# Attention times value in four 32-column tiles, two attention visits per group, and the projections reordered around them

## The chip, the cores and the metric

The kernel runs on one core of a Trainium2 chip, in true float32. The metric is the device time of one execution, in microseconds (us). TensorE is the matrix engine; VectorE (DVE), ScalarE (ACT) and GpSimd (POOL) work beside it.

## The reference, cut to what matters

Two layers on 64 graphs of 256 nodes and 512 features, each layer with a norm, a ReLU and a residual. The first mixes nodes with the adjacency matrix, the second is masked attention with 8 heads of 64.

```python
# layer 0
h = jnp.maximum(_layernorm(x), 0.0)
y = jnp.einsum('nm,bmd->bnd', adj, h)
x = x + jnp.einsum('bnd,do->bno', y, weight) + bias
# layer 1
h = jnp.maximum(_layernorm(x), 0.0)
q, k, v = ...                                   # h @ Wq + bq etc., 8 heads of 64
scores = jnp.einsum('bqhd,bkhd->bhqk', q, k) / sqrt(64)
scores = scores + (1.0 - adj) * -1e9
attn = jax.nn.softmax(scores)
out = jnp.einsum('bhqk,bkhd->bqhd', attn, v)
x = x + out @ Wo + bo
```

## The kernel before

It takes two graphs at a time: 32 groups, one after the other, software-pipelined by hand. The names in the profile are `py` (adjacency times h), `w` (layer 0's projection), `ph` (transposes of h), `q`, `k`, `v`, `sc` (scores), `pav` (attention times value), `pden` (the softmax denominators, a matmul with ones) and `o` (the output projection, called post). Group numbers stand in the names: `o_9a` is bank a of group 9's post.

A projection is done by a seven-product scheme on halves: five projections, seven products each, eight passes of TensorE for each product. It steps through its products, and other work is put between the steps. The order of `read` and `finish` in it, which are adds on VectorE for `w` and `o`, decides when an accumulation bank comes free:

```python
def project(s, halves, by_token, name, read, finish):
    pa = new("a")
    product(pa, s, "a11", halves, "b11", by_token, stop=False)   # first product
    u1 = read(pa, 1)                                             # w, o: residual add
    yield
    ...                                                          # second product, bank b
    product(pa, s, "s2", halves, "t2", by_token, start=False, stop=False)  # third, into pa again
    u2 = read(pa, 2)
    yield
    pc = new("c")
    product(pc, s, "s1", halves, "t1", by_token, stop=False)
    yield
    product(pa, s, "s3", halves, "t3", by_token, start=False)
    u3 = read(pa, 3)              # w, o: two residual adds
    give(pa)
    finish(pc, u3, 1, 1)
    yield
    ...                           # sixth product, bank d
    product(pc, s, "s4", halves, "b22", by_token, start=False)   # last: waits for finish(pc)
```

Attention goes by pairs of heads, so four times per group. `attend` uses two 64-column tiles of TensorE for a pair; behind it stand the scores of the next pair, and that whole stretch (`pav`, `pden`, `sc`) I call a visit.

```python
def attend(g, hp):
    po = bank([P, GN], f"pav_{g}_{hp}")
    pd = bank([P, GN], f"pden_{g}_{hp}")
    for b in range(GB):
        for k in range(NT):
            for j in range(2):
                h = 2 * hp + j
                nc.tensor.matmul(po[j * HD:(j + 1) * HD, b * N:(b + 1) * N], V..., a[:, j * NT + k, :], ...)
    for b in range(GB):
        for j in range(2):
            nc.tensor.matmul(pd[j * HD:(j + 1) * HD, b * N:(b + 1) * N], ones, s[:, j, :], ...)
    ...
    nc.scalar.activation(den, pd, AF.Identity, accum_out=stats[:, 0, i:i + 1])   # frees pd
    def invert(c):                                                               # four times
        nc.vector.reciprocal(rden[:, c * P:(c + 1) * P], den[:, c * P:(c + 1) * P])
    def divide():
        nc.vector.tensor_tensor(o, po, rden, op=ALU.mult)
    for c in range(4):
        after(1 + c, invert, c)       # so many steps later, among other work
    after(5, divide)

SHARE = (11, 3, 12, 7)                # steps of the next group's layers behind each visit
for g in range(NG):
    for hp in range(4):
        attend(g, hp)
        score(g, hp + 1)              # or score(g + 1, 0)
        ...                           # behind visit 1: post(g - 1)
        for _ in range(steps):
            run(layers)
```

## Time and profile before

| what | before |
|---|---|
| median time | 2965.51 us (2964.91 to 2967.16) |
| TensorE busy | 98% |
| period of a group, from `py` to the next `py` | 90.3 us |
| one visit: `pav` + `pden` + `sc` | 1.78 + 0.96 + 1.93 us |
| start: until `py` of group 2 begins | 189.8 us |
| end: from `py` of group 31 | 156.0 us |

An engine's row in the profile gives its busy time, its share of the span and its number of instructions. In the timeline each row is a block of equal instructions: start, duration, engine, source line, operation and tiles, shapes, count, and in brackets how long the engine stood idle before the block and whose instruction ended that. Ends of matmuls are modelled, so the cost of a block is the distance from its start to the next start. The chain is the work that ended last, followed back step by step to what released it. A weight load is exposed when no running matmul covers it, as at 1020.29 us in this profile: the load for `w_11c` begins 0.25 us after the last matmul ended, and the second pass starts 0.32 us after the first, where those behind it stand 0.216 apart. The prediction below shows the rows.

### The profile page before, as it was taken

The page shows a single profiled execution, that of the slowest core. Times are in us where ns is not written, and L with a number is a line of the kernel's source. Part 1 is how long each engine was busy: PE and PEld are TensorE (multiplying, and loading weights), DVE is VectorE, ACT ScalarE, POOL GpSimd, SP SyncE. Part 2 cuts the span into 40 slices and gives each one's busy share as a digit, 9 for nine tenths or more (in the row PEclk, how much of TensorE's full clock was granted, in tenths as well). Part 3 has the DMA queues.
Part 4 walks back from the last instruction along what each step waited for, and adds up shares of the span by engine and source line. Part 5 has one row for each costly group of instructions (what it writes and reads, how often), then busy time and mean ns, then how long its engine had stood idle before and what let it go on. Part 6 is the DMA issues. An engine that isn't in the chain of part 4 may idle for free.

```text
span 2964.6 us, 39918 instructions
## 1 busy us (share of the span) xinstructions
PE 2896.8 (98%) x15632; PEld 2341.8 (79%) x15632; DVE 1698.0 (57%) x2959; ACT 942.4 (32%) x1697; POOL 1886.4 (64%) x1754
## 2 busy tenths in 40 slices
PE   7899999999999999999999999999999999999997
PEld 6688788878887887888888888888878878888885
DVE  3465556555555655555555556555556555665554
ACT  2233333333323333333333233333333333333331
POOL 6566656666666666566666666665666665666653
PEclk9899999999999999999999999999999999999998
DMA  3000000000000000000000000000000000000000
GB/s 125 1 1 29 29 29 29 15 15 29 29 29 29 1 29 29 29 29 24 6 29 29 29 29 5 25 29 30 29 29 1 29 29 29 29 14 16 29 15 30
DMA packets 39279, 75.74 MB, mean 26 GB/s; under 512 B 3248, under 2 KB 3504, under 8 KB 39088
## 3 DMA queue, kind: packets, MB, share of 16 engines
q1 hardware_dynamic: 39088, 73.15, 6.9%
q8 instruction: 125, 2.05, 0.3%
q14 instruction: 66, 0.54, 0.1%
HBM read 39.59 MB, written 33.55 MB: 25 GB/s over the span
## 4 chain that ended last, share of the span: by engine, by line
PE 93%; DVE 5%; POOL 1%; issue 0%; ACT 0%; DMA 0%; SPq 0%; ACTq 0%; POOLq 0%; DVEq 0%
PE sc L587 8%; PE pav L618 8%; PE py L469 8%; DVE x L424 4%; PE pden L624 4%; PE ph L511 2%; PE q_1a L383 0%; POOL a L595 0%; DVE rden L637 0%; DMA adj_sb<-in_adj_dram 0%; PE q_31a L383 0%; PE q_30a L383 0%; PE q_23a L383 0%; PE q_20a L383 0%; PE q_19a L383 0%
## 5 line engine op out<-in xcount | busy, mean ns | idle before, releaser
L595 POOL TENSOR_TENSOR a<-a,top 128x1024 f32<-128x1024 f32 x256 | 598.5, 2359 | 342.9 <-DVE a L592 342.9
L592 DVE SCALAR_TENSOR_TENSOR a<-sc,maskT 128x512 f32<-128x512 f32 x512 | 318.1, 684 | 370.1 <-PE sc L587 370.1
L637 DVE RECIPROCAL rden<-den 128x128 f32<-128x128 f32 x512 | 453.1, 922 | 5.2 <-ACT den L633 5.2
L607 POOL TENSOR_TENSOR as<-a 128x512 f32<-128x512 f32 x256 | 322.9, 1273 | 33.0 <-ACT a L604 33.0
L53 POOL TENSOR_TENSOR rs<-rs,mhalf 128x2 f32<-128x2 f32 (+1 forms) x96 | 77.6, 808 | 416.4 <-DVE nb L52 416.4
L604 ACT ACTIVATE a<-a 128x1024 f32<-128x1024 f32 x256 | 266.4, 1053 | 122.5 <-POOL a L595 122.5
L618 PE MATMUL pav<-a,v 128*64 128x256 f32 x2048 | 256.8, 392 | 15.1 <-ACT a L604 15.1
L587 PE MATMUL sc<-q,k 64*128 64x256 f32 x2048 | 257.9, 392 | 0.0
L587 PEld LDWEIGHTS sc<-q,k 64*128 64x128 f32 x2048 | 188.9, 188 | 67.6 <-PE pden L624 36.9
L376 POOL TENSOR_TENSOR t_h<-h1T 128x256 f32<-128x256 f32 x128 | 92.9, 726 | 230.4 <-DVE h1T L513 230.1
L469 PE MATMUL py<-adjT,h 128*128 128x256 f32 x1024 | 231.4, 384 | 6.7 <-ACT h L441 6.7
L633 ACT ACTIVATE den<-pden 128x512 f32<-128x512 f32 x128 | 75.8, 592 | 489.5 <-PE pden L624 489.5
L618 PEld LDWEIGHTS pav<-a,v 128*64 128x64 f32 x2048 | 136.8, 138 | 118.5 <-issue 52.6
L469 PEld LDWEIGHTS py<-adjT,h 128*128 128x128 f32 x1024 | 192.9, 191 | 42.6 <-issue 10.3
L501 ACT ACTIVATE h<-x,nb,rs 128x512 f32<-128x512 f32 x128 | 97.2, 807 | 366.5 <-POOL nb L54 366.5
L443 POOL TENSOR_TENSOR x<-x,b_r 128x512 f32<-128x512 f32 x128 | 161.5, 1273 | 0.3 <-ACT h L441 0.3
L524 POOL TENSOR_TENSOR x<-x,bo_r 128x512 f32<-128x512 f32 x128 | 159.8, 1269 | 0.0
L471 ACT COPY yT<-py 128x512 f32<-128x512 f32 x128 | 75.1, 586 | 209.9 <-PE py L469 209.9
L624 PE MATMUL pden<-as,ones 128*64 128x256 f32 x1024 | 135.7, 384 | 3.5 <-POOL as L607 3.5
L624 PEld LDWEIGHTS pden<-as,ones 128*64 128x64 f32 x1024 | 78.1, 139 | 38.4 <-POOL as L607 4.4
L441 ACT ACTIVATE h<-x,nb,rs 128x512 f32<-128x512 f32 x128 | 102.8, 806 | 6.4 <-POOL nb L54 6.4
L376 POOL TENSOR_TENSOR t_y<-yT,t_y 128x256 f32<-128x256 f32 x128 | 93.3, 729 | 15.4 <-ACT yT L471 12.8
(2950 smaller groups left out, 5766.4 us busy)
## 6 DMA issues: line engine op xcount, KB each, us to landing
x<-in_x_dram SPq DMA_DIRECT2D x32, 1024.0 KB, 5.3
out_dram<-x SPq DMA_DIRECT2D x64, 512.0 KB, 2.8
w_sb<-in_L_gnn_weight_dram SPq DMA_DIRECT2D x1, 1024.0 KB, 8.0
wq_sb<-in_L_gnn_Wq_dram SPq DMA_DIRECT2D x1, 1024.0 KB, 11.4
wk_sb<-in_L_gnn_Wk_dram SPq DMA_DIRECT2D x1, 1024.0 KB, 13.3
wv_sb<-in_L_gnn_Wv_dram SPq DMA_DIRECT2D x1, 1024.0 KB, 10.9
wo_sb<-in_L_gnn_Wo_dram SPq DMA_DIRECT2D x1, 1024.0 KB, 8.9
adj_sb<-in_adj_dram SPq DMA_DIRECT2D x1, 256.0 KB, 5.9
```

The lines of the kernel that those rows point to most:

```text
L376: eng.tensor_tensor(self.t[n][:, c, :], self.operand(p, c), self.operand(q, c), op=ALU.subtract)
L443: nc.gpsimd.tensor_tensor(xt[:, t, :], xt[:, t, :], b0_r, op=ALU.add)
L469: nc.tensor.matmul(ps[:, b * N:(b + 1) * N], h[:, b * NT + k, d * P:(d + 1) * P], adjT[:, k, :], start=(k == 0), stop=(k == NT - 1))
L524: nc.gpsimd.tensor_tensor(xt[:, t, :], xt[:, t, :], bo_r, op=ALU.add)
L587: nc.tensor.matmul(ps[j][:, kt * N:(kt + 1) * N], k[j * HD:(j + 1) * HD, c, kt * P:(kt + 1) * P], q[j * HD:(j + 1) * HD, c, :], start=True ...
L592: nc.vector.scalar_tensor_tensor(a[:, j * NT:(j + 1) * NT, :].rearrange("p k n -> p (k n)"), ps[j], SCALE, maskT_f, op0=ALU.mult, op1=ALU.add)
L595: nc.gpsimd.tensor_tensor(a, a, top_b, op=ALU.subtract)
L604: nc.scalar.activation(a, a, AF.Exp)
L607: nc.gpsimd.tensor_tensor(s, a4[:, :, 0, :], a4[:, :, 1, :], op=ALU.add)
L618: nc.tensor.matmul(po[j * HD:(j + 1) * HD, b * N:(b + 1) * N], V[g][h // 4, b][:, k, (h % 4) * HD:(h % 4 + 1) * HD], a[:, j * NT + k, :], ...
L624: nc.tensor.matmul(pd[j * HD:(j + 1) * HD, b * N:(b + 1) * N], ones, s[:, j, :], start=True, stop=True)
L637: nc.vector.reciprocal(rden[:, c * P:(c + 1) * P], den[:, c * P:(c + 1) * P])
```

## The change

Its intent: TensorE is the bound, so use its columns better. Four heads (a quad) are worked on at once, each in a tile of 32 columns, and the 64 columns of a head are taken in two halves. Attention then comes twice per group instead of four times. The denominators need one row of 32 ones per head instead of 64. `Wo` and the value bias are loaded in the order of rows that this leaves. The projections are split into `layer0`, `queries_keys`, `values` and `post`, and laid between the two visits. In `project` the add that frees bank c moves ahead of one of the residual adds. Not shown below: the first input comes in four pieces, and in the last post the fourth product comes second (`first_half_first`), with GpSimd's sums in a new order. The core of the diff:

```diff
-    def attend(g, hp):
-        po = bank([P, GN], f"pav_{g}_{hp}")
...
+    def attend(g, qd):
+        po = [bank([P, GN], f"pav_{g}_{qd}_{f}") for f in range(2)]
+        pd = bank([P, GN], f"pden_{g}_{qd}")
         for b in range(GB):
+            v = V[g][qd, b]
+            for k in range(NT):
+                for f in range(2):
+                    for h in range(4):
+                        nc.tensor.matmul(po[f][h * 32:(h + 1) * 32, b * N:(b + 1) * N],
+                                         v[:, k, h * HD + f * 32:h * HD + f * 32 + 32],
+                                         A[h // 2, b][:, (h % 2) * NT + k, :],
+                                         start=(k == 0), stop=(k == NT - 1), tile_position=(0, h * 32))
         for b in range(GB):
+            for h in range(4):
+                nc.tensor.matmul(pd[h * 32:(h + 1) * 32, b * N:(b + 1) * N], ones[:, 0:32], AS[h // 2, b][:, h % 2, :],
+                                 start=True, stop=True, tile_position=(0, h * 32))
...
     # project()
         u3 = read(pa, 3)
+        finish(pc, u3, 1, 1)
+        read(pa, 4)               # the second residual add, w and o only
         give(pa)
-        finish(pc, u3, 1, 1)
...
+    score(0, 0); run(values(0)); run(layer0(1))       # lines joined here
     for g in range(NG):
+        attend(g, 0)
+        score(g, 1)
+        run(post(g - 1))                              # conditions on g cut
+        run(queries_keys(g + 1))
+        attend(g, 1)
+        score(g + 1, 0)
+        run(values(g + 1))
+        run(layer0(g + 2))
```

## The prediction

> **What bounds the kernel now.** I read the page first: the busy shares, then the slices, then the chain that ended last.
>
> ```profile
> span 2964.6 us, 39918 instructions
> PE 2896.8 (98%) x15632; PEld 2341.8 (79%) x15632; DVE 1698.0 (57%) x2959; ACT 942.4 (32%) x1697; POOL 1886.4 (64%) x1754
> ...
> PEclk9899999999999999999999999999999999999998
> ...
> PE 93%; DVE 5%; POOL 1%; issue 0%; ACT 0%; DMA 0%; SPq 0%; ACTq 0%; POOLq 0%; DVEq 0%
> ...
> L618 PE MATMUL pav<-a,v 128*64 128x256 f32 x2048 | 256.8, 392 | 15.1 <-ACT a L604 15.1
> L624 PE MATMUL pden<-as,ones 128*64 128x256 f32 x1024 | 135.7, 384 | 3.5 <-POOL as L607 3.5
> ```
>
> TensorE is busy 98% at full clock and is 93% of the chain, so only what shortens TensorE's own stream counts; VectorE's 57% matters only where TensorE waits for it. "x2048" counts two passes for each float32 matmul (the program has 1024). Then I read the timeline of TensorE in a steady stretch.
>
> ```profile
> 1016.43 1.89 PE L383 MATMUL w_11a<-w_sb,t_y 128*128 128x256 f32 x8
> 1018.15 1.89 PE L383 MATMUL w_11d<-w_sb,t_y 128*128 128x256 f32 x8
> 1020.30 1.99 PE L383 MATMUL w_11c<-w_s,yT 128*128 128x256 f32 x8 [0.25 <-DVE x L424]
> 1022.22 1.95 PE L618 MATMUL pav<-a,v 128*64 128x256 f32 x16
> 1024.00 1.03 PE L624 MATMUL pden<-as,ones 128*64 128x256 f32 x8
> 1024.96 2.00 PE L587 MATMUL sc<-q,k 64*128 64x256 f32 x16
> 1026.89 1.99 PE L383 MATMUL o_9a<-wo_sb,oT 128*128 128x256 f32 x8
> 1028.72 1.89 PE L383 MATMUL o_9b<-wo_sb,oT 128*128 128x256 f32 x8
> ```
>
> Read starts, not durations. A product of 8 full passes takes 1018.15 - 1016.43 = 1.72 us: 215.7 ns a pass, which I call a slot. 16 passes of pav (64 columns) take 1.78 us, hence two in each slot, side by side. The period is 90.30 us per group (py of layer 0 starts at 1002.51 and 1092.81). My sum: 280 projection passes 60.40, py 6.90, transposes 1.97, scores 6.90, pav 6.90, pden 3.45 = 86.5 us. The rest is pauses, read from start times in the trace: (a) each change of the array's shape costs about 93 ns before and 51 to 105 ns behind the first pass, about 0.2 us, three times in each of four attention visits; with an 0.08 us hitch inside pav a visit costs 0.62, hence 2.5 us; (b) the last product of the w and o projections stands 0.52 us late twice ([0.25 <-DVE x L424], and an exposed weight load); (c) 0.2 us twice in q and k. 86.5 + 2.5 + 1.04 + 0.4 = 90.4, against 90.30 measured.
>
> [...] The trace shows two instructions per matmul, each 215.7 ns for 256 columns[...]. [...] the prediction hangs on it: in the built program both passes of one matmul stand in front of the other tile's, yet the first passes of both column tiles start 7 ns apart, and each tile goes on at its own 215.7 ns. [...] No run here shows four.
>
> **The change part by part.**
> 1. Attention times value. Four heads at 32 columns instead of two at 64: passes per group go from 64 to 128. At four per slot that is again 32 slots, 6.90 us. Gain 0.
> 2. Denominators. One row of 32 ones for each head instead of 64: still 32 passes, but four per slot: 8 slots instead of 16. Gain 8 x 0.2157 = 1.73 us.
> 3. Two visits of twice the size instead of four. Today one visit is 1022.22 to 1026.89, 4.67, plus 0.09 before and 0.105 behind: 4.87; four are 19.5. A new one is 36 slots (16 pav, 4 pden, 16 scores), 7.77, plus three changes of shape, 0.53: 8.30; two are 16.6. Gain of parts 1 to 3 together 2.9 us per group.
> 4. In w and o, the add that frees the c bank moves ahead of one residual add. VectorE's adds start 0.60 us apart; today the bank is free about 0.35 us after the pass could start, so then 0.25 us before: the pause goes. Gain 2 x 0.52 = 1.04 us.
> 5. Reciprocals: 512 to 256 of 922 ns, 227 us less of VectorE; ACT loses half its den copies. Beside TensorE: worth nothing directly.
> 6. A new wait. Scores now send eight evictions (0.60 us apart, the first 1.23 us after the scores' start) and one reciprocal (0.86) ahead of post's first residual add: it starts at about 1.23 + 8 x 0.60 + 0.86 = 6.9 us and frees the bank at 7.57; TensorE wants to accumulate there at 7.21. With the exposed weight load a loss of 0.47 us per group. Behind the other score stands v, which ScalarE evicts: no wait.
> Period: 90.30 - 2.9 - 1.04 + 0.47 = 86.87 us.
> 7. Start. Today py of group 2 starts at 189.76; from 15 us on that stretch is 174.76 us, of which TensorE is busy 157.57 at a mean clock of 0.94. Its pauses (3.5 for as, 3.2 for a, 5.4 for h1T, and passes at low clock behind each) come from short cover between score and attend. The new order puts v and layer 0 of group 1 between them (31 us). Work to the same point is about 139.5 us; with first py at 15.5 and 8 us left of pauses: 163. Splitting the first load gains nothing: the adjacency then lands later.
> 8. End, from the start of group 31's v (2881.9): today 82.7 us, with waits of 6.83, 4.16 and 3.89. Mine: v 12.1, attend 4.4 + 3.5 waiting for the last key sums, scores 3.7, post 12.6, attend 4.6, last post 15 (with 2.5 of waits), output 6: 62. From py of group 31: 86.87 - 12.1 + 62 = 136.8, today 156.
> Sum: 163 + 29 x 86.87 + 136.8 = 2819. Predicted 2820 us, 4.9% less.
>
> **The rivals.**
> A. Four column tiles do not run four abreast. For it: a tile's two passes stand together in the program, so four first passes need reordering over six passes, where two tiles needed it over two[...]. Against it: the pairs in this trace already overtake. If only two run, attention times value and denominators need 80 slots instead of 40: +8.6 us per group, +276 in all: about 3095. If four streams merely slow each other, to 300 ns a slot: 40 x 0.084 = 3.4 us per group, about 2925.
> B. Bank shortage. Attend holds three of eight banks, and the scores want eight. But the order of release gives the fourth pair the banks of the first, evicted at about 2.0 and 2.6 us, and TensorE gets there at 2.7. If it binds, 0.5 us per visit: +32, 2850.
> C. POOL's chain comes late at attend. Four subtractions of 2.36, eight output sums of 0.73 and four key sums of 1.27 end about 23 us after the scores began; v and layer 0 give 35. It binds only at the end, as counted.
> D. Gain hidden anyway (POOL 64%, DVE 57% already idle enough): against it speaks TensorE's 98%. If only the start and end gained: about 2920.
>
> **Range and chances.** A in full about 0.1, A in part about 0.1; otherwise 2790 to 2860, as start and end are uncertain by 15 us and B or small waits by 30. Range 2785 to 2895. Faster by over 2% means under 2905.9: 0.86; within 2%: 0.04; slower: 0.10.
>
> **What would show it.** In the timeline, a pav visit with 64 passes in about 3.45 us and pden with 16 in 0.87 confirm parts 1 and 2; 6.9 and 1.7 would be rival A. The period between two py starts should be 86.9; w's and o's last product without its [<-DVE x] bracket; one about 0.4 us in front of post's third product, named DVE x, and DVE reciprocals at about 235 us busy. First py of group 2 near 163. A period over 89, or waits named DVE a in the scores (B) or POOL as (C), would make me wrong.

## The result, and the profile after

The changed kernel takes 2841.05 us (median of 4 runs, 2840.43 to 2842.41) against 2965.51 of the kernel before in the same rounds. The ratio is 0.958, with a 95% interval of 0.9564 to 0.9597. (Such a ratio is the mean time of one kernel's fast runs over the mean of the other's of the same rounds, so not quite the ratio of the medians quoted.) The result is correct. It is 21 us above the predicted 2820 and inside the range.

First the page of the changed kernel: the span, the busy times, the chain that ended last, and two groups (busy us, mean ns of one, idle before).

```profile
span 2840.6 us, 43306 instructions
...
PE 2799.5 (99%) x17680; PEld 2301.5 (81%) x17680; DVE 1478.2 (52%) x2703; ACT 851.7 (30%) x1441; POOL 1882.6 (66%) x1754
...
PE 96%; POOL 2%; DVE 1%; issue 1%; DMA 0%; ACT 0%; SPq 0%; DVEq 0%; POOLq 0%; ACTq 0%
...
L638 PE MATMUL pav<-a,v 128*32 128x256 f32 x4096 | 234.3, 381 | 0.0
L656 DVE RECIPROCAL rden<-den 128x128 f32<-128x128 f32 x256 | 231.8, 926 | 4.6 <-ACT den L652 4.6
```

The group of reciprocals that the last row answers to, in the kernel before:

```profile
L637 DVE RECIPROCAL rden<-den 128x128 f32<-128x128 f32 x512 | 453.1, 922 | 5.2 <-ACT den L633 5.2
```

TensorE is the bound as much as ever (99% busy, 96% of the chain), with 2048 more `pav` passes than before and a shorter span: more passes, and more of them at once. The reciprocals are halved in number at the same 0.92 us, as the prediction counted, and VectorE's share of the chain falls from 5% to 1%.

Then TensorE's timeline over one visit and the post behind it, in the changed kernel:

```profile
1067.95 1.94 PE L394 MATMUL w_12c<-w_s,yT 128*128 128x256 f32 x8
1069.82 3.66 PE L638 MATMUL pav<-a,v 128*32 128x256 f32 x64
1073.30 1.05 PE L644 MATMUL pden<-as,ones 128*32 128x256 f32 x16
1074.28 4.09 PE L608 MATMUL sc<-q,k 64*128 64x256 f32 x32
1078.29 1.99 PE L394 MATMUL o_10a<-wo_sb,oT 128*128 128x256 f32 x8
1080.12 1.89 PE L394 MATMUL o_10b<-wo_sb,oT 128*128 128x256 f32 x8
1081.85 1.99 PE L394 MATMUL o_10a<-wo_s,t_o 128*128 128x256 f32 x8
1083.67 1.89 PE L394 MATMUL o_10c<-wo_s,t_o 128*128 128x256 f32 x8
```

64 passes of `pav` take 1073.30 - 1069.82 = 3.48 us, which is 16 slots of 215.7 ns (3.45): four passes in a slot. `pden` takes 0.98 for 16 passes. In the trace the first passes of the four tiles start 0, 7, 14 and 20 ns after the first one, the next four 240 to 260 ns, and from there on each tile goes on every 215.7 ns. The `w` product in front of the visit has lost its `[0.25 <-DVE x L424]`. One thing is out of place: these 32 score passes take 4.01 us, while those of the other visit take 3.65.

The difference, by stage (from the starts of `py`; 29 periods lie between groups 2 and 31):

| stage | before | after | gained | predicted after |
|---|---|---|---|---|
| until `py` of group 2 | 189.76 | 180.12 | 9.6 | 163 |
| one period | 90.305 | 87.047 | 3.26, times 29 = 94.5 | 86.87 |
| from `py` of group 31 | 156.0 | 136.2 | 19.8 | 136.8 |
| span of the profiled run | 2964.6 | 2840.6 | 124.0 | 2819 |

One such period, in TensorE's timeline of the changed kernel (87.03 us from start to start):

```profile
963.59 7.07 PE L480 MATMUL py<-adjT,h 128*128 128x256 f32 x32
...
1050.62 7.07 PE L480 MATMUL py<-adjT,h 128*128 128x256 f32 x32
```

So a period came out 0.2 us longer than predicted and the end 0.6 us shorter. 17 of the missing 21 us are in the start, 5 in the 29 periods. At the end, 15.2 us of waits (11.3 for ScalarE's `a`, 3.9 for a check on VectorE) became 4.1; no experiment takes the end apart.

**The start.** The view of TensorE's waits in the first 180 us of the changed kernel, behind the first `py` (in all us, how often, longest us):

```profile
PE ph L525 <- ACT h L512: 3.3, 1, 3.3
PE pbo L348 <- issue: 3.1, 1, 3.1
PE q_1a L394 <- POOL t_h L387: 2.9, 2, 2.1
PE v_0c L394 <- POOL a L616: 2.0, 1, 2.0
PE q_1a L394 <- DVE h1T L527: 1.7, 1, 1.7
```

These are 13.0 us. They cost more than that, as TensorE's timeline there shows:

```profile
130.53 1.89 PE L394 MATMUL q_1b<-h1T,wq_sb 128*128 128x256 f32 x8
134.51 0.70 PE L394 MATMUL q_1a<-t_h,wq_s 128*128 128x256 f32 x2 [2.09 <-POOL t_h L387]
136.00 2.93 PE L394 MATMUL q_1a<-t_h,wq_s 128*128 128x256 f32 x6 [0.79 <-POOL t_h L387]
138.72 3.51 PE L394 MATMUL q_1c<-t_h,wq_s 128*128 128x256 f32 x8
```

`q_1b` has no wait and is followed after 3.98 us, of which 2.09 is the wait behind it. Then `q_1c`, with all its data there, needs 142.06 - 138.72 = 3.34 us for the eight passes that take 1.73 elsewhere. The view by windows gives the granted clock for that stretch (after the window: TensorE's busy time, weight loads, VectorE, ScalarE, GpSimd, clock):

```profile
136.00:142.00 6.00, 6.00 (x14) 4.83 (x15) 0.00 (x0) 3.04 (x6) 5.70 (x7) 0.50 0.00 0
```

Half speed for six microseconds behind a pause of two and a short one. The same stands at `ph` (granted clock 0.57) and behind the wait of `v_0c` (0.54 for 3.4 us); behind the 3.1 us in front of `pbo` the clock stayed at 1.00. The trace's clock record has half speed from 43.00 to 46.41, 94.20 to 97.61 and 135.16 to 141.98; from its beginning at 22.52 us to there, the stretches at full and at half speed are 20.48, 3.41, 47.79, 3.41, 37.55 and 6.83 us long, each a multiple of 3.41. In the 3.41 us before each stretch at half speed, TensorE was busy for 0.55, 1.43 and 1.32 us; in the two such stretches that share the pause in front of `pbo` (53.24 to 56.65 and on to 60.06) it was busy for 2.02 and 1.75, and the clock stayed. So the length of a pause alone does not tell what was lost: 3.1 us in front of `pbo` cost no clock, 2.0 in front of `v_0c` did. What decides it these runs don't show. The first passes of `py` also take twice their time: they start every 0.43 us until 22.5 us and every 0.216 from there. The clock record begins only at 22.52 us, and the view shows the time before it as full speed, so 1.00 there is no measurement. Counted over the whole start from the trace, behind the first `py` at 16.8 us, each block by the distance to the next start: the passes at full speed are 136.5 us, changes of shape and a held score 4.6, waits 12.9, and slow passes 9.3 (`ph` 1.9, `v_0c` 1.6, `q_1a` 1.4, `q_1c` 1.6, `py` 2.7).

**The late scores.** ScalarE's timeline, then VectorE's, around the visit shown above:

```profile
1074.23 1.52 ACT L512 ACTIVATE h<-x,nb,rs 128x512 f32<-128x512 f32 x2 [0.36 <-POOL nb L54]
1075.65 0.57 ACT L652 ACTIVATE den<-pden 128x512 f32<-128x512 f32 x1
```

```profile
1075.51 4.87 DVE L613 SCALAR_TENSOR_TENSOR a<-sc,maskT 128x512 f32<-128x512 f32 x8 [2.29 <-PE sc L608]
1080.30 0.94 DVE L656 RECIPROCAL rden<-den 128x128 f32<-128x128 f32 x1
1081.16 0.62 DVE L441 TENSOR_TENSOR x<-o_10a,x 128x512 f32<-128x512 f32 x1
```

The scores want eight banks in turn. One of them is the bank of the denominators, which ScalarE frees by its copy `den<-pden`. That copy stands behind two activations of layer 0, so it comes at 1075.65 to 1076.2, and the third pair of scores waits for it: 0.36 us. On VectorE the eight evictions and one reciprocal stand ahead of post's first residual add, as predicted; but because TensorE is itself late by 0.36 us, only 0.10 of that wait is left (the second `o_10a` begins its successor 1.82 instead of 1.72 us later). Together 0.46 us per group.

### The profile page after: what moved, and what is told of

The parts are those of the page before. It is cut to its first block, busy times and chain, and to the rows that moved or that the text cites.

```text
span 2840.6 us, 43306 instructions
## 1 busy us (share of the span) xinstructions
PE 2799.5 (99%) x17680; PEld 2301.5 (81%) x17680; DVE 1478.2 (52%) x2703; ACT 851.7 (30%) x1441; POOL 1882.6 (66%) x1754
## 4 chain that ended last, share of the span: by engine, by line
PE 96%; POOL 2%; DVE 1%; issue 1%; DMA 0%; ACT 0%; SPq 0%; DVEq 0%; POOLq 0%; ACTq 0%
PE sc L608 8%; PE py L480 8%; PE pav L638 8%; PE pden L644 2%; PE ph L525 2%; POOL a L616 1%; DVE x L441 0%; DVE a L613 0%; DMA adj_sb<-in_adj_dram 0%; PE q_0a L394 0%; PE o_25a L394 0%; PE o_17a L394 0%; PE o_5a L394 0%; PE o_7a L394 0%; PE o_4a L394 0%
## 5 line engine op out<-in xcount | busy, mean ns | idle before, releaser
L613 DVE SCALAR_TENSOR_TENSOR a<-sc,maskT 128x512 f32<-128x512 f32 x512 | 311.9, 681 | 230.1 <-PE sc L608 230.1
L608 PE MATMUL sc<-q,k 64*128 64x256 f32 x2048 | 250.1, 384 | 0.0
L608 PEld LDWEIGHTS sc<-q,k 64*128 64x128 f32 x2048 | 205.3, 186 | 45.5 <-PE pden L644 25.5
L512 ACT ACTIVATE h<-x,nb,rs 128x512 f32<-128x512 f32 x128 | 97.2, 806 | 460.6 <-POOL nb L54 460.6
L638 PE MATMUL pav<-a,v 128*32 128x256 f32 x4096 | 234.3, 381 | 0.0
L656 DVE RECIPROCAL rden<-den 128x128 f32<-128x128 f32 x256 | 231.8, 926 | 4.6 <-ACT den L652 4.6
L638 PEld LDWEIGHTS pav<-a,v 128*32 128x32 f32 x4096 | 126.5, 110 | 98.2 <-issue 21.2
L458 ACT ACTIVATE h<-x,nb,rs 128x512 f32<-128x512 f32 x128 | 96.4, 806 | 11.0 <-POOL nb L54 11.0
L504 DVE BATCH_NORM_STATS2 st<-x 128x6 f32<-128x256 f32 x256 | 96.4, 419 | 4.4
L387 POOL TENSOR_TENSOR t_o<-oT,t_o 128x256 f32<-128x256 f32 x128 | 93.3, 743 | 7.8 <-DVE oT L660 7.8
L387 POOL TENSOR_TENSOR t_h<-h1T,t_h 128x256 f32<-128x256 f32 x128 | 92.8, 725 | 5.0
```

What stands on the lines that cost most here:

```text
L387: eng.tensor_tensor(self.t[n][:, c, :], self.operand(p, c), self.operand(q, c), op=ALU.subtract)
L512: nc.scalar.activation(h1[:, k * NT + t, :], xt[:, k * NT + t, :], AF.Relu, bias=nb[:, t:t + 1], scale=rs[:, t:t + 1])
L608: nc.tensor.matmul(ps[j][:, kt * N:(kt + 1) * N], k[j * HD:(j + 1) * HD, c, kt * P:(kt + 1) * P], q[j * HD:(j + 1) * HD, c, :], start=True ...
L613: nc.vector.scalar_tensor_tensor(a[:, j * NT:(j + 1) * NT, :].rearrange("p k n -> p (k n)"), ps[j], SCALE, maskT_f, op0=ALU.mult, op1=ALU.add)
L638: nc.tensor.matmul(po[f][h * 32:(h + 1) * 32, b * N:(b + 1) * N], v[:, k, h * HD + f * 32:h * HD + f * 32 + 32], A[h // 2, b][:, (h % 2) * ...
```

## The experiments

The result agreed with the prediction's total, which doesn't show that its parts are right. The theory to be tested is the prediction's own: the gain is the packing of the denominators by four, two visits instead of four, and the moved add; attention times value gains nothing; a VectorE wait in post takes 0.47 back. The rivals: the four tiles are not what pays but the new order with its longer cover (and reciprocals halved as a side effect); and the lost half microsecond belongs to ScalarE's copy and a bank (near to B), not to VectorE. Periods below are read from the starts of `py` as above.

**1. The moved add alone, in the kernel before.**

```diff
         u3 = read(pa, 3)
-        give(pa)
         finish(pc, u3, 1, 1)
+        read(pa, 4)
+        give(pa)
-    RESIDUAL = {1: [(0, 0)], 2: [(0, 1)], 3: [(1, 1), (1, 0)]}
+    RESIDUAL = {1: [(0, 0)], 2: [(0, 1)], 3: [(1, 1)], 4: [(1, 0)]}
```

> The kernel before, with only part 4 of the change: the add that frees the c bank moved ahead of one residual add. If my accounting holds, the bracket of 0.25 us in front of the last product of w and o is gone, the period between two py starts falls by 1.04 us from 90.30 to about 89.26, and the time falls by about 33 us to about 2932. If the rival holds, that the gain of the whole change is mostly this order and the narrow tiles give nothing, the time comes near 2870.

Measured: 2937.79 us (2937.40 to 2937.93), ratio 0.9905 (0.9888 to 0.9921), correct. The period is 89.36, 0.94 less, and the bracket in front of the last product of `w` and `o` is gone. A two-line change in the order of adds on an engine that is 57% busy is worth 28 us.

**2. The same undone in the changed kernel.**

```diff
         u3 = read(pa, 3)
-        finish(pc, u3, 1, 1)
         read(pa, 4)
         give(pa)
+        finish(pc, u3, 1, 1)
```

> The changed kernel with part 4 alone undone. Expected: the pause in front of the last product of w and o comes back, 0.5 us twice per group, a period of about 88.05 us and about 2873 us. If in the new order VectorE has slack there, because its reciprocals are halved, the time stays near 2841.

Measured: 2869.26 us (2867.17 to 2870.53), ratio 0.9671 (0.9655 to 0.9687), correct. The period is 0.93 longer than the changed kernel's, and the wait is back. TensorE's timeline of this kernel, the third and the last product of one post:

```profile
1002.04 1.99 PE L394 MATMUL o_9a<-wo_s,t_o 128*128 128x256 f32 x8 [0.19 <-DVE x L441]
...
1009.47 1.99 PE L394 MATMUL o_9c<-wo_s,oT 128*128 128x256 f32 x8 [0.25 <-DVE x L441]
```

So part 4 is worth the same in both settings: it adds up with the rest. By accident this run shows something else too. The banks come free in another order here, the scores are not held (3.65 us), and the lost time stands in post's third product, where the prediction had put it.

**3. Two tiles of 64 columns in the new order.** This keeps quads, two visits and all else, and takes away the four tiles. The reciprocals then double again. To fit into memory the output buffers went from 6 to 4 and the guard's sums cover only half of the heads, both on purpose.

```diff
-                for f in range(2):
-                    for h in range(4):
-                        nc.tensor.matmul(po[f][h * 32:(h + 1) * 32, b * N:(b + 1) * N], ...)
+                for c in range(2):
+                    for j in range(2):
+                        nc.tensor.matmul(po[c][j * HD:(j + 1) * HD, b * N:(b + 1) * N], ...)
...
         def invert(c):
-            nc.vector.reciprocal(rden[:, c * P:(c + 1) * P], den[:, c * P:(c + 1) * P])
+            for f in range(2):
+                nc.vector.reciprocal(rden[f][:, c * P:(c + 1) * P], den[f][:, c * P:(c + 1) * P])
```

> The changed kernel with its quads, its two visits and its order of work, but with tiles of 64 columns: two heads side by side, two banks of denominators, reciprocals doubled again. If the narrow tiles are what pays in the denominators, pden takes 8 slots more per group (1.73 us), and a fourth bank held by attend may add up to 0.9 us of waits in the scores: a period of 88.8 to 89.7 us against 87.03, and 2896 to 2925 us against 2841. If the order of work alone made the gain, the time stays within 10 us of 2841.

Measured: 3014.66 us (3014.29 to 3014.74), ratio 1.0164 (1.0147 to 1.0181), correct. The new order without the four tiles is slower than the kernel before. TensorE's timeline:

```profile
1035.67 1.90 PE L639 MATMUL pden<-as,ones 128*64 128x256 f32 x16
1037.50 3.72 PE L602 MATMUL sc<-q,k 64*128 64x256 f32 x32
...
1045.88 1.99 PE L388 MATMUL o_9a<-wo_s,t_o 128*128 128x256 f32 x8 [1.00 <-DVE x L435]
```

The period is 92.58, 5.53 more than the changed kernel's. `pden` takes 1.83 instead of 0.98 us, 1.7 per group. The other 3.8 are new waits with the late passes behind each, and every wait in the list for this period names VectorE: 1.0 in front of post's third product, 0.7 and 0.4 further on in it, 1.2 in `v`. In this kernel two reciprocals (1.75 us, in its VectorE timeline) stand between the evictions and each of post's adds, where the changed kernel has one. So the order with its cover does not gain by itself: that rival falls, though this run doesn't say what the order would be worth with VectorE out of the way. And the prediction's "worth nothing directly" for the reciprocals does not carry over: in the quad order halving them keeps VectorE off the path. The changed buffers are a second difference in this run; that no wait names anything but VectorE speaks against them, but doesn't exclude them.

**4. The same passes, head by head** (one look).

```diff
-            for k in range(NT):
-                for f in range(2):
-                    for h in range(4):
+            for h in range(4):
+                for k in range(NT):
+                    for f in range(2):    # eight passes of one tile in a row
```

> The changed kernel with attention times value issued head by head: eight passes in a row for one column tile before the next tile's come, instead of two. It measures how far ahead of a waiting tile TensorE takes up another tile's passes. If [...]the look-ahead reaches eight passes and more, pav stays at 3.5 us for 64 passes and the time at 2841. If it reaches only across the second pass of one matmul, the four tiles run one after another: up to 48 slots more in each of 64 visits, some 10 us per visit, and the time can rise by up to 660 us. Anything in between tells the depth.

Measured: 3126.75 us, a single run, correct. TensorE's timeline:

```profile
1027.24 7.52 PE L638 MATMUL pav<-a,v 128*32 128x256 f32 x61
1034.39 0.42 PE L644 MATMUL pden<-as,ones 128*32 128x256 f32 x3
...
1035.03 0.38 PE L638 MATMUL pav<-a,v 128*32 128x256 f32 x1
1035.06 1.21 PE L644 MATMUL pden<-as,ones 128*32 128x256 f32 x7
1036.20 3.73 PE L608 MATMUL sc<-q,k 64*128 64x256 f32 x32
```

All 64 passes of `pav` are there: 61 in a row and three among the first of `pden`, which start ahead of them. The 61 alone take 7.15 us, where the changed kernel needs 3.48 for 64, and from the start of `pav` to the scores it is 8.96 us instead of 4.46: 61 passes in 33 slots, so about two tiles run abreast, not four. Twice these 4.5 us are the 9.0 by which the period is longer (96.04). The starts show it too. The trace does not name the tile, but one tile starts a pass every 216 ns, so a pass that starts sooner is another tile's. The first such pass begins 894 ns after the first of the visit, 6 ns behind the fifth of the first tile's eight passes (888; the text of experiment 5 has 4 ns): five of the eight have started by then, three have not. The same step comes again 893 ns later, at 1787. What holds the other tile until then, the trace does not show.

**5. Four passes of one tile in a row** (one look). In experiment 4 another tile began just behind the fifth pass of the first, so four in a row should still pack: an estimate of mine from that one start.

```diff
-                for f in range(2):
-                    for h in range(4):
+                for h in range(4):
+                    for f in range(2):
```

> The changed kernel with four passes in a row for one column tile before the next tile's (the changed kernel has two, the head by head run eight). In the head by head run the next tile's first pass started 4 ns behind the fifth of eight[...]. Then four in a row fit: after the first four tiles have started, pav still takes 3.5 to 3.7 us for 64 passes and the time is 2841 to 2855. If the reach is less, pav takes 5 us or more and the time is over 2930.

Measured: 2847.18 us, a single run, correct. `pav` takes 3.48 us (1031.42 to 1034.90), with the four first passes at 0, 13, 26 and 40 ns; the period is 87.21 (`pden` takes 0.07 us longer each time). So with four passes of a tile in a row `pav` loses nothing (3.48 us for 64 passes), and with eight it does (7.15 for 61). Between four and eight I did not measure.

**6. The denominators twice** (each computed two times over, same result).

```diff
-        for b in range(GB):
+        for _, b in [(r, b) for r in range(2) for b in range(GB)]:
             for h in range(4):
```

> The changed kernel with the denominators' matmuls issued twice (the second time over the first, same values), nothing else. It measures them by themselves. If 16 passes of 32 columns take four slots and lie wholly on the path, each visit grows by 0.86 us, the period from 87.03 to 88.76, the time to about 2896. It also gives the key sums, VectorE and the banks more time, so up to 0.3 us per group of the waits in the scores can go with it. If the denominators were hidden, the time stays at 2841.

Measured: 2895.04 us (2893.94 to 2897.12), ratio 0.9764 (0.9749 to 0.9779), correct. TensorE's timeline:

```profile
1047.25 1.91 PE L644 MATMUL pden<-as,ones 128*32 128x256 f32 x32
1049.09 3.72 PE L608 MATMUL sc<-q,k 64*128 64x256 f32 x32
```

The period grows by 1.72 us for 32 more passes, eight slots by count, 1.73 us. Slots of this kind are on the path at their full price, with nothing hidden. So taking eight away was worth 1.7 per group, some 54 us in all (2895.04 - 2841.05), as part 2 has it. The scores beside post are not held here (3.65 us); the same 0.36 us stands in front of post's third product instead.

**7. The copy of the denominators on VectorE** instead of ScalarE, which frees their bank early. The guard's sum on ScalarE moves to the end of the division.

```diff
-        nc.scalar.activation(den, pd, AF.Identity, accum_out=stats[:, 0, i:i + 1])
+        nc.vector.tensor_copy(den, pd)
         give(pd)
...
+            nc.scalar.activation(den, den, AF.Identity, accum_out=stats[:, 0, i:i + 1])   # in divide()
```

> The changed kernel with the denominators copied out of their bank by VectorE, which is idle at that point, instead of by ScalarE behind two activations of layer 0. The scores beside post then take 3.65 us instead of 4.01. But my account of the new wait says it only moves: VectorE's first residual add still starts 6.9 us after the scores' start, so post's third product now waits 0.46 us. Period 87.0 within 0.15, time 2841 within 5. If the bank was the wait's only cause, the period falls by 0.36 and the time to about 2829.

Measured: 2848.82 us (2847.29 to 2850.05), ratio 0.9607 (0.9592 to 0.9622), correct; slower than I expected by about 8 us. The scores are freed as expected, from 4.01 to 3.65 us, which shows that the bank held them. But TensorE's timeline shows where it went:

```profile
1079.72 1.89 PE L394 MATMUL o_10b<-wo_sb,oT 128*128 128x256 f32 x8
1081.81 1.99 PE L394 MATMUL o_10a<-wo_s,t_o 128*128 128x256 f32 x8 [0.20 <-DVE x L441]
```

Post's third product now stands 0.36 us late (2.09 for 1.72): the wait moved from the bank to VectorE's residual add. `v`'s last product is late as well (1.91 for 1.73), so the period is 0.24 longer than before this edit. The two waits in the changed kernel are one behind the other, and removing the first only uncovers the second.

**8. That, and the reciprocals one step later,** behind post's first residual add instead of ahead of it.

```diff
         for c in range(4):
-            after(1 + c, invert, c)
-        after(5, divide)
+            after(2 + c, invert, c)
+        after(6, divide)
```

> The same, and the reciprocals and the division one step later, so that post's first residual add stands ahead of the first reciprocal on VectorE. Now both causes are gone: the scores take 3.65 us and post's third product starts without a wait. Period 86.55, time about 2827. If the wait has a third cause, it stays at 2841.

Measured: 2828.20 us (2828.00 to 2830.08), ratio 0.9540 (0.9527 to 0.9553), correct. The same place in TensorE's timeline:

```profile
1067.41 3.73 PE L608 MATMUL sc<-q,k 64*128 64x256 f32 x32
1071.07 1.99 PE L394 MATMUL o_10a<-wo_sb,oT 128*128 128x256 f32 x8
1072.90 1.89 PE L394 MATMUL o_10b<-wo_sb,oT 128*128 128x256 f32 x8
1074.62 1.89 PE L394 MATMUL o_10a<-wo_s,t_o 128*128 128x256 f32 x8
```

Scores 3.66, then 1.83, then 1.72: both waits are gone. The period is 86.60, 0.45 less than the changed kernel's, which is the whole of what the prediction's new wait took back.

**9. The start.** Weight sums of `Wo` and part of layer 0 of group 1 are moved to where TensorE has other work.

```diff
+    run(first, 2)
     out_bias()
...
-    WO = weight_sums(nc.gpsimd, wo_sb, "wo")
-    run(layer0(1))
+    held = layer0(1)
+    run(held, 6)                  # the rest behind score(0, 1)
...                                # Wo's sums: inside queries_keys(1)
```

> The changed kernel with its first 180 us mended alone: the output bias product two steps later (it waits 3.1 us for the weights of the output projection, which now come in eight pieces), the sums of those weights off POOL's path to the first scores (2.0 us of wait and low clock behind it), and the last five products of layer 0 of group 1 held back between the second scores and the projections that wait for POOL and VectorE there (4.5 us, and low clock behind). If these waits are why the start took 180 us and not the 163 I predicted, py of group 2 starts at 166 to 171 us, the period stays 87.0, and the time is about 2830. If the start is bound by something else, say POOL's total work, it stays near 178 to 180 and 2841.

Measured: 2836.36 us (2835.55 to 2837.07), ratio 0.9564 (0.9549 to 0.9579), correct. `py` of group 2 begins at 173.72, 6.4 us earlier, and not in the 166 to 171 expected: partly a miss. (The medians are 4.7 us apart; the profiled run of the changed kernel was the slowest of its four.) Two rows of the waits in this kernel's start (in all us, times, longest):

```profile
PE ph L525 <- ACT h L512: 8.4, 3, 3.9
PE pbo L348 <- issue: 1.2, 1, 1.2
```

The waits for GpSimd and VectorE are gone, but the transposes now wait three times for ScalarE's `h`, 8.4 us for 3.3 before. In the first 180 us the chain from one layer to the next has little other work to lie beside.

**10. Experiments 8 and 9 together.** The edit is both diffs.

> The mended start together with VectorE's copy of the denominators and the later reciprocals. The two gains lie in different stretches and should add: period 86.6, py of group 2 near 168, time 2816 to 2820. It would be faster than both kernels.

Measured: 2826.12 us (2826.02 to 2827.93), ratio 0.9530 (0.9517 to 0.9543), correct, the lowest median of all. The gains do not add up: `py` of group 2 is at 176.34, with the waits for `h` at 8.0 and others back (2.0 for `pbo`, 1.5 for `h1T`), and the sum stays 6 us or more above what I expected. Against experiment 8 it is 2 us, the intervals of the two overlap, and they were measured on two chips, so which of them is better is not shown. Both are faster than the changed kernel and the kernel before.

**11. Scores split in halves in both visits,** with one step of the following projection between, on top of experiment 8. It asks what a change of the array's shape costs, and whether the longer cover is needed.

```diff
-        score(g, 1)
+        score(g, 1, (0,))
+        between = post(g - 1) if g > 0 else iter(())
+        run(between, 1)
+        score(g, 1, (1,))
...
-            score(g + 1, 0)       # the same with values(g + 1)
```

> The kernel with the later reciprocals (2828 us, no waits left in the visits), with one projection product between the two halves of every score block: nothing added but two more changes of the array's shape per visit, 126 in all. By my figure of 0.2 us for each this costs 0.4 us per visit, 0.8 us per group: a period of 87.4 and about 2853 us. If a change of shape were free once the next weights are ready, the time stays at 2828.

Measured: 2882.12 us (2881.72 to 2883.01), ratio 0.9717 (0.9702 to 0.9732), and the result is wrong, with a relative error of 0.0326. This was not intended: by the schedule, in the last group the split takes a step away and attend comes ahead of its last key sum. The rest of the schedule is the same, so the steady periods can still be read: 88.28, 1.69 more than experiment 8. The split itself is about 0.39 us for each visit, 0.78 in all; the remaining 0.9 stand at `w`'s third product, which waits 0.72 us for GpSimd's `t_y`. GpSimd works without a gap from the scores to there.

**12. The split beside post only,** which leaves that chain alone and gives a correct result.

> The split scores again, mended: only the score block beside post is split by one product, where GpSimd has slack and the last group's key sums are issued in time (the run before gave a wrong result because the last attend came one step ahead of its last key sum, and it had a wait for POOL of 0.7 us in w that I had not counted). Two more changes of shape per group, 62 in all. At 0.2 us each: a period of 86.6 + 0.4 = 87.0 and about 2840 us, against 2828 without the split. If a change of shape costs nothing, 2828; if the 1.7 us per group of the run before were all shape, 0.85 here and 2853.

Measured: 2841.50 us (2840.48 to 2842.37), ratio 0.9579 (0.9566 to 0.9592), correct. Its TensorE timeline:

```profile
1073.14 2.00 PE L608 MATMUL sc<-q,k 64*128 64x256 f32 x16
1075.07 1.99 PE L394 MATMUL o_10a<-wo_sb,oT 128*128 128x256 f32 x8
1077.00 2.00 PE L608 MATMUL sc<-q,k 64*128 64x256 f32 x16
1078.92 1.99 PE L394 MATMUL o_10b<-wo_sb,oT 128*128 128x256 f32 x8
```

The first three blocks, eight slots each (1.73 us by count), take 1.93, 1.93 and 1.92. The period is 86.98, 0.38 more than experiment 8's, for two more changes of shape: 0.19 us each. So two visits instead of four pay by the changes that they avoid.

## Why the prediction was right or wrong, point by point

- **Part 1, no gain from `pav`: right.** Twice 3.48 us against three times 1.78 and once 1.83 is 0.2 us, and that belongs to the fewer visits. Rival A falls: four tiles run four abreast (64 passes in 16 slots). Its worry about the order of the program was the right one, but it comes true later than it feared: with four passes of a tile in a row `pav` still takes 3.48 us (experiment 5), with eight 61 passes take 7.15 (experiment 4).
- **Part 2, denominators 1.73 us: right.** Experiment 6 gives 1.72 for as many slots.
- **Part 3, with 1 and 2 together 2.9 us: right.** Inside the visits three times 4.67 and once 4.75 (18.76) became 8.11 and 8.47, of which 0.36 is the wait, so 16.22 without it: 2.54 us. Two visits fewer also spare the late product at each of their edges, four times about 0.09 us in the two timelines, which makes 2.9. Experiment 12 gives the price of a change of shape independently: 0.19 us.
- **Part 4, 1.04 us: right in cause, a tenth too large.** Experiments 1 and 2: 0.94 and 0.93.
- **Part 5, the reciprocals "worth nothing directly": wrong in the new order.** Experiment 3, where the quad order runs with all the reciprocals, loses some 3.8 us per group to waits, which the trace puts down to VectorE. The prediction looked at VectorE's average of 57%, and had in its own part 6 the place where the adds are late. It did no harm to the number, as the change does halve them.
- **Part 6, a new wait of 0.47 us: right in size (0.46), wrong in cause for 0.36 of it.** 0.36 of it is a bank that ScalarE frees late, which rival B had considered only for the banks of the scores themselves. Behind it, and hidden by it, stands the wait that was predicted: experiment 7 removes the bank and finds the other, and experiment 8 removes both and gets 0.45 us.
- **Sum of the period.** 90.31 - 2.9 - 0.94 + 0.46 = 86.93, against 87.05 measured and 86.87 predicted. The rest of 0.12 is `w`'s third product, followed after 1.79 instead of 1.73 us, and the transposes, 1.98 instead of 1.91; experiment 11 shows the first waiting for GpSimd when pressed. Rival C was right to look at GpSimd, and it is next in line. Rival D falls by the period itself, which is 3.26 us shorter. Two slips in the prediction's sums cost little: its own terms add up to 86.83, not 86.87, and a visit of 4.87 us stands 0.56 above its 20 slots, not 0.62; the hitch inside `pav` is in one visit of the four only, with 0.05 us (1.83 for 1.78).
- **Part 7, start at 163 us: the term that was mis-sized.** It was 15.5 for the first `py`, 139.5 of work and 8 of pauses. Measured are 16.8 (with the first load split, the adjacency landed at 8.8 us instead of 7.1), 141.1 (136.5 + 4.6) and 22.2 (12.9 of waits, 9.3 of slow passes). Work and cause were right, the pauses were put at a third of what they are. The prediction had listed "passes at low clock behind each" pause and then wrote one figure that doesn't even cover the waits. The new order covers group 1's attention; it does not cover group 0's chain through the norms, and experiment 9 could only move those waits.
- **Part 8, end 136.8 us: right,** 136.2 measured, and by its parts too: the last `attend` behind `v` takes 7.0 instead of 7.9 us, as it waits 1.7 for the last key sums where 3.5 was written, and no other part is more than half a microsecond off.

## What to carry to other kernels

With TensorE as the bound, count array slots (215.7 ns here) and changes of its shape (0.19 us each here). Matmuls that fill only some columns packed four to a slot here as long as the passes of the different tiles stood close together in the program: with two or four passes of a tile in a row 64 took 3.48 us, with eight 61 took 7.15. Look for waits where an engine with a low average share has its work in a burst: one add moved by one place was 28 us of the 124 here, and a copy and the reciprocals moved after it another 13. Where two waits end at nearly the same time, removing one uncovers the other, so move both before you judge; and count a pause at the start with the slow passes that may stand behind it: here 12.9 us of waits and 9.3 of slow passes, though none behind the 3.1 us in front of `pbo`.
